# Weighted sums of rows moved from VectorE to TensorE, with the rows loaded back from DRAM

## The chip, the cores and the metric

The kernel runs on one core of one Trainium2 chip. The metric is the device time of one execution in microseconds (us). The engines are called by the profile's letters: PE is TensorE (matrix products and transpositions), DVE is VectorE, ACT is ScalarE, POOL is GpSimd, SP is SyncE, which issues most of the transfers (DMA).

## The reference, cut to what matters

Two transformer layers work on 4 sequences of 512 tokens with 512 features, in float32. The first layer normalizes each row (a row is a token) and gives the result, `xn`, to an attention and to a mixture of experts. This attention has a local window and a compressed memory. The change lies in the making of the compressed memory:

```
w_log   = (xn @ Wcmp + bcmp).reshape(B, C, 4)          # C = 128 groups of 4 tokens
w_cmp   = softmax(w_log, axis=-1)
entries = einsum('bcr,bcrh->bch', w_cmp, xn.reshape(B, C, 4, 512))
ck = apply_rope(rmsnorm(entries @ Wk + bk, kn_w), block_ends)
cv = entries @ Wv + bv
sc = einsum('bhsd,bcd->bhsc', q, ck) * scale            # top 8 of these are attended to
```

Every group of four successive tokens gets four weights that add up to 1, and an entry is the weighted sum of the four rows. From the entries come compressed keys `ck` and values `cv`, 128 for each sequence, which all 16 heads of that sequence use.

## The kernel before

The first layer is a loop of 32 steps (L1020): 8 groups of two heads, and for each group the 4 sequences, here called batches. A step makes the scores and the context of its two heads and at the same time the projections of the next step. `project` (L638) makes these with seven products of half matrices in the place of eight; their sums and differences of blocks are made by DVE and POOL and, for the first four steps, stored to DRAM as `xsd` (L656). Products land in banks of PSUM, which are asked for by tag: three banks are `mm` (projections `p`, outputs `op`), three `sc` (scores, `st`, contexts, the product `wB`), two `tr` (transpositions).

`start_sequence` (L871) normalizes a block of 128 rows: `bn_stats` on DVE, a power on POOL, the scaled rows `xn` on DVE or ACT. It stores `xn` to the DRAM tensor `xnd` (L237; blocks 4 to 7 from ACT's queue, the others from SP's), and turns it by TensorE into `xnT`, which has the features in the partitions (L242, L243). The first batch's four blocks are made ahead of the loop, the second batch's too, the third's in step 0 and the fourth's in step 1. `layernorm` pins the statistics of blocks 0 to 3 to their place in the order (L219).

`compress(b, pool)` (L578) is a generator in four parts, run for batch 0 ahead of the loop (L1007 to L1018) and for batches 1 to 3 in steps 0 to 2 at four places each (L885). Its input `row_w[b]` holds the logits, made by `first_logits` in four column blocks of 32 (L252) and copied to `lr` by ACT (L254).

- Part 1 turns the logits (`wt`), makes the softmax of four (`w1`), and spreads it: `wd[:, :, r]` is the identity times the weight of token r of the group (four DVE instructions, L596).
- Part 2 multiplies `wd` by a matrix of ones (L599), so that bank `wB` holds all 512 weights in every partition. Then for each of the 4 blocks of features DVE multiplies `xnT` by `wB` (L603) and adds up each four neighbours (L604) into `entT`, features in the partitions.
- Part 3 makes keys and values from `entT` in eight products (`kv`, L609), normalizes and rotates the keys.
- Part 4 turns the keys (`trck`, L619) into `ckT` (L620), which the scores `sp` of the step need (L744).

The order of each engine's instructions is made when the kernel is built, from the order of the program and from the build's own estimate of when each instruction can start; what stands in `keep_in_program_order` keeps its place. At run time every engine and every queue works strictly in its order: an instruction that waits holds up all behind it. That the build changes the order can be seen in the trace: the stores of row blocks 8 and 9, written in step 0 behind the four stores of that step's sums, stand ahead of them on SP's queue.

The setup tiles (pool `sp0`, compression's tiles among them) are released after the last compression, at the end of step 2 (L891); the routing of the experts takes their place and starts in step 3.

Of the kernel before, what the change touches and what calls it, by code (L numbers as in the profile page):

```python
# [12 lines left out]
F32 = mybir.dt.float32  # L13
I32 = mybir.dt.int32
AF = mybir.ActivationFunctionType
ALU = mybir.AluOpType
AX = mybir.AxisListType
# [3 lines left out]
P = 128  # L21
B, S, HID = 4, 512, 512
T = B * S
NT = T // P
TC = S // P
KC = HID // P
NH, D = 16, 128
RATIO = 4
C = S // RATIO
# [20 lines left out]
def two_layers(ctx: ExitStack, tc: tile.TileContext, a: dict, out: bass.AP, large: bass.AP):  # L50


    FEW = 32
    nc = tc.nc
    V, G, A, PE = nc.vector, nc.gpsimd, nc.scalar, nc.tensor
# [14 lines left out]
    sp0 = setup.enter_context(tc.tile_pool(name="setup", bufs=2, side="right"))  # L70


    def psum(tag, name):
        return ps.tile([P, 512], F32, tag=tag, name=name, bufs={"mm": 3, "sc": 3, "tr": 2}[tag])
# [53 lines left out]
    xnT = keep.tile([P, KC, T], F32, tag="xnT", name="xnT")  # L128
    x_v = a["x"].rearrange("(n p) h -> p n h", p=P)

    xnd = dram.tile([T, HID], F32, tag="xnd", name="xnd")
# [43 lines left out]

    ident = const.tile([P, P], F32, tag="ident", name="ident")
    make_identity(nc, ident)
    nhalf = const.tile([P, 8], F32, tag="nhalf", name="nhalf")
    G.memset(nhalf, -0.5)
    A.activation(small.tile([P, 8], F32, tag="warm", name="warm", bufs=1), nhalf, AF.Exp)  # L180
    ones_sq = const.tile([P, P], F32, tag="ones_sq", name="ones_sq")
    G.memset(ones_sq, 1.0)
# [376 lines left out]
    def squares(x, n, pool, name, extra=1.0):  # L559

        sq = pool.tile([P, D], F32, tag="sq", name=f"sq_{name}", bufs=1)
        ss = small.tile([P, n], F32, tag=f"ss{n}", name=f"ss_{name}", bufs=4)
        for h in range(n):
            A.activation(sq, x[:, h, :], AF.Square, accum_out=ss[:, h : h + 1])  # L564
        G.tensor_scalar(ss, ss, D * 1e-6, extra, ALU.add, ALU.mult)
        G.tensor_tensor(ss, ss, nhalf[:, 0:n], ALU.pow)  # L566
        return ss

    def rotate(x, tt1, tt2, n, pool, name):

        r1 = pool.tile([P, n, R], F32, tag="r1", name=f"r1_{name}", padded_shape=[P, 6, R] if n > 1 else None, bufs=1)
        r2 = pool.tile([P, n, R], F32, tag="r2", name=f"r2_{name}", padded_shape=[P, 6, R] if n > 1 else None, bufs=1)
        V.tensor_tensor(r1, x[:, :, 0:R], tt1, ALU.mult)
        V.tensor_tensor(r2[:, :, 0:32], x[:, :, 32:R], tt2[:, :, 0:32], ALU.mult)
        V.tensor_tensor(r2[:, :, 32:R], x[:, :, 0:32], tt2[:, :, 32:R], ALU.mult)
        V.tensor_tensor(x[:, :, 0:R], r1, r2, ALU.add)

    def compress(b, pool):  # L578

        w_row = row_w[b]  # L580

        wt = psum("tr", f"wt_{b}")
        for r in range(RATIO):
            PE.transpose(wt[:, ts(r, P)], w_row.rearrange("p (c r) -> p r c", r=RATIO)[:, r, :], ident)
        w1 = pool.tile([P, RATIO], F32, tag="w1", name=f"w1_{b}", bufs=1)
        V.tensor_reduce(w1, wt.rearrange("p (r k m) -> p r k m", k=KC, m=FEW)[:, :, :, 0], AX.X, ALU.add)
        V.tensor_scalar(w1, w1, bcmp[:, 0:1], None, ALU.add)
        mx = pool.tile([P, 1], F32, tag="wmx", name=f"wmx_{b}", bufs=1)
        V.tensor_reduce(mx, w1, AX.X, ALU.max, negate=True)
        sm = pool.tile([P, 1], F32, tag="wsm", name=f"wsm_{b}", bufs=1)  # L590
        A.activation(w1, w1, AF.Exp, bias=mx, accum_out=sm)
        V.reciprocal(sm, sm)
        V.tensor_scalar(w1, w1, sm, None, ALU.mult)
        wd = pool.tile([P, C, RATIO], F32, tag="prod", name=f"wd_{b}", bufs=1)
        for r in range(RATIO):
            V.tensor_scalar(wd[:, :, r], ident, w1[:, r : r + 1], None, ALU.mult)  # L596
        yield
        wB = psum("sc", f"wB_{b}")
        PE.matmul(wB, lhsT=ones_sq, rhs=wd.rearrange("p c r -> p (c r)"), start=True, stop=True)  # L599
        entT = pool.tile([P, KC, C], F32, tag="entT", name=f"entT_{b}", bufs=1)  # L600
        for k in range(KC):
            prod = pool.tile([P, C, RATIO], F32, tag="prod", name=f"prod_{b}_{k}", bufs=1)
            V.tensor_tensor(prod.rearrange("p c r -> p (c r)"), xnT[:, k, ts(b, S)], wB, ALU.mult)  # L603
            V.tensor_reduce(entT[:, k, :], prod, AX.X, ALU.add)  # L604
        yield
        kv = psum("sc", f"kv_{b}")
        for i, w in enumerate((wk, wv)):
            for k in range(KC):
                PE.matmul(kv[:, ts(i, D)], lhsT=entT[:, k, :], rhs=w[:, k, :],  # L609
                          start=(k == 0), stop=(k == KC - 1))  # L610
        V.tensor_tensor(cv[:, b, 0:D], kv[:, ts(1, D)], bkv[:, 1, :], ALU.add)
        ck = pool.tile([P, 1, D], F32, tag="ck", name=f"ck_{b}", bufs=1)
        V.tensor_tensor(ck[:, 0, :], kv[:, ts(0, D)], bkv[:, 0, :], ALU.add)
        ss = squares(ck, 1, pool, f"ck_{b}")
        rotate(ck, t1c, t2c, 1, pool, f"ck_{b}")
        A.activation(ck[:, 0, :], ck[:, 0, :], AF.Copy, scale=ss[:, 0:1])
        yield
        tr = psum("tr", f"trck_{b}")
        PE.transpose(tr[:, 0:C], ck[:, 0, :], ident)  # L619
        A.activation(ckT[:, b, :], tr[:, 0:C], AF.Copy, scale=turned[:, 0:1])  # L620
        yield
# [231 lines left out]
    lg0 = lg1 = const.tile(full, F32, tag="lg", name="lg")  # L853
    row_w = {}
    comp = [compress(b, sp0) for b in range(B)]

    def first_logits(b):
# [581 lines left out]
    for g in range(NG):  # L1439
        b, j = groups1[g]  # L1440
# [743 lines left out]
```

## Time and profile before

| what | value |
| --- | --- |
| median of 3 runs (lowest to highest) | 2073.92 us (2073.34 to 2074.24) |
| the profiled execution | 2074.66 us |
| its span in the profile | 2072.6 us |
| mean granted clock of TensorE | 0.995 |
| DMA | 267.23 MB, 129 GB/s in the mean |
| first and last `wt` (the first instruction of compression) | 27.5 and 158.0 us |
| first and last `kv` | 49.3 and 185.6 us |
| `xnd<-xn` from SP and from ACT, to landing | 2.0 and 2.2 us (median) |

The profile shows one execution by the hardware's own records. The page gives each engine's busy time, the span in 40 slices and the costliest groups of instructions. Queries of the trace give windows (busy time of every engine, granted clock of TensorE and share of the DMA engines in a stretch of time), timelines (start, length, instruction and, in brackets, the idle time before it with what ended it), tiles (every instruction that reads or writes a tile) and the chain of waits (followed back from the last instruction). A float32 product is two passes on TensorE, a transposition is one; pipelined instructions overlap in the lists, so the cost of one is better read from the start of the next.

### The profile page before, as it was taken

How to read it: one execution, taken by the hardware profiler on the slowest of the kernel's cores; microseconds unless marked ns; L12 is line 12 of the kernel's file. 1: busy time of each engine (PE TensorE's matmuls, PEld its weight loads, DVE VectorE, ACT ScalarE, POOL GpSimd, SP SyncE). 2: the span in 40 equal slices, each digit the busy share in tenths (PEclk: the TensorE clock that was granted, in tenths of full speed). 3: DMA queues.
4: the chain of work that ended last, by engine and by line, in shares of the span. 5: the costliest groups of instructions: out<-in, count | busy, mean ns of one | idle time of the engine just before them, and what ended most of it. 6: DMA issues, size and time to landing. Idle time of an engine off the chain costs nothing.

```text
span 2072.6 us, 27984 instructions
## 1 busy us (share of the span) xinstructions
PE 2017.7 (97%) x9130; PEld 1205.3 (58%) x9130; DVE 1452.0 (70%) x3543; ACT 867.9 (42%) x2600; POOL 754.3 (36%) x761
## 2 busy tenths in 40 slices
PE   6999999999999999999999999999999999999997
PEld 4666666666666666666666666666334445445442
DVE  7888967666766666676667778787596555557775
ACT  4554444444444443444444455454243432333332
POOL 4422244443423333344333444353114332332550
PEclk9999999999999999999999999999999999999999
DMA  7102133333333343234443222121317765773551
GB/s 250 68 31 62 42 118 120 143 108 103 130 130 104 109 155 103 92 135 166 183 170 116 70 76 85 42 72 62 119 51 244 263 243 196 257 243 123 158 163 52
DMA packets 98906, 267.23 MB, mean 129 GB/s; under 512 B 14400, under 2 KB 27840, under 8 KB 87488
## 3 DMA queue, kind: packets, MB, share of 16 engines
q0 software_dynamic: 27072, 148.91, 21.4%
q1 hardware_dynamic: 70528, 114.34, 16.4%
q10 hardware_dynamic: 1152, 2.10, 0.3%
q8 instruction: 75, 1.23, 0.2%
q14 instruction: 79, 0.65, 0.1%
HBM read 222.05 MB, written 42.73 MB: 128 GB/s over the span
## 4 chain that ended last, share of the span: by engine, by line
PE 81%; DVE 8%; ACT 3%; POOL 2%; DMA 2%; issue 1%; SPq 0%; ACTq 0%; POOLq 0%; DVEq 0%
PE p L661 23%; PE hp_r L518 12%; PE op L828 10%; PE st L753 4%; PE st L1224 3%; PE qp L1200 3%; PE sp L744 3%; PE cx L1238 2%; PE ca L797 2%; PE o L1307 2%; PE trm_r L506 2%; PE vp L1160 1%; PE trq L681 1%; PE trk L687 1%; PE cc L800 1%
## 5 line engine op out<-in xcount | busy, mean ns | idle before, releaser
L828 PE MATMUL op<-Wo,cT 128*128 128x512 f32 x512 | 230.6, 598 | 5.3 <-DVE lv L725 2.9
L518 PE MATMUL hp_r<-we_r,xT_r 128*128 128x512 f32 (+1 forms) x592 | 224.8, 596 | 0.0
L470 POOL DMA_INDIRECT xr_r<-xnd,rows_r x72 | 89.4, 1242 | 331.6 <-PE trm_r L506 298.2
L761 POOL TENSOR_TENSOR lT<-lT,lmask 128x512 f32<-128x512 f32 (+1 forms) x128 | 157.6, 1244 | 140.8 <-ACT lT L757 140.6
L661 PE MATMUL p<-wT,x 128*128 128x384 f32 x512 | 179.6, 493 | 0.5 <-DVE wT L119 0.5
L661 PE MATMUL p<-wB,x 128*128 128x384 f32 x512 | 175.9, 488 | 4.0 <-DVE u L717 4.0
L661 PE MATMUL p<-wA,xnT 128*128 128x384 f32 x512 | 174.0, 492 | 0.2 <-DVE u L696 0.2
L828 PEld LDWEIGHTS op<-Wo,cT 128*128 128x128 f32 x512 | 92.0, 190 | 115.0 <-issue 77.2
L564 ACT ACTIVATE sq<-qb 128x128 f32<-128x128 f32 x384 | 118.9, 310 | 93.0 <-DVE qb L710 44.9
L1226 ACT ACTIVATE pT<-st 128x1024 f32<-128x1024 f32 x128 | 123.7, 1014 | 62.7 <-PE st L1224 57.0
L518 PEld LDWEIGHTS hp_r<-we_r,xT_r 128*128 128x128 f32 (+1 forms) x592 | 83.8, 170 | 97.3 <-issue 91.8
L831 DVE TENSOR_TENSOR acc<-acc,op 128x512 f32<-128x512 f32 x128 | 87.4, 685 | 69.4 <-PE op L828 69.0
L661 PEld LDWEIGHTS p<-wB,x 128*128 128x128 f32 x512 | 93.9, 190 | 68.5 <-issue 10.2
L661 PEld LDWEIGHTS p<-wT,x 128*128 128x128 f32 x512 | 94.5, 193 | 63.5 <-issue 6.7
L661 PEld LDWEIGHTS p<-wA,xnT 128*128 128x128 f32 x512 | 95.6, 193 | 61.0 <-issue 2.9
L675 ACT ACTIVATE qb<-qb,ss 128x128 f32<-128x128 f32 x256 | 81.9, 390 | 110.7 <-POOL ss L566 108.6
L508 ACT COPY xT_r<-trm_r 128x512 f32<-128x512 f32 x72 | 41.8, 581 | 198.0 <-PE hp_r L518 188.3
L757 ACT ACTIVATE lT<-st,ss 128x256 f32<-128x256 f32 (+1 forms) x128 | 47.2, 449 | 175.4 <-PE st L753 175.3
L753 PE MATMUL st<-qkT 128*128 128x256 f32 (+1 forms) x512 | 110.4, 357 | 0.0
L534 POOL DMA_INDIRECT row_r<-yd,slot_r x64 | 74.2, 1160 | 94.0 <-DVE row_r L1341 35.8
L753 PEld LDWEIGHTS st<-qkT 128*128 128x128 f32 x512 | 93.1, 193 | 11.4 <-issue 1.4
L566 POOL TENSOR_TENSOR ss<-ss,nhalf 128x6 f32<-128x6 f32 x64 | 95.7, 1496 | 5.3
(360 smaller groups left out, 4334.2 us busy)
## 6 DMA issues: line engine op xcount, KB each, us to landing
x<-xsd SPq DMA_DIRECT2D x112, 256.0 KB, 3.1
yd<-yr_r SPq DMA_DIRECT2D x72, 256.0 KB, 3.4
wA<-in_wA SPq DMA_DIRECT2D x16, 384.0 KB, 3.6
wB<-in_wB SPq DMA_DIRECT2D x16, 384.0 KB, 7.6
xnd<-xn SPq DMA_DIRECT2D x24, 256.0 KB, 2.0
accd<-acc SPq DMA_DIRECT2D x18, 256.0 KB, 2.0
acc<-in_x SPq DMA_DIRECT2D x16, 256.0 KB, 4.9
Wo<-in_Wo SPq DMA_DIRECT2D x8, 512.0 KB, 3.6
```

The source lines that it names most:

```text
L470: G.indirect_dma_start(out=out, out_offset=None, in_=src, in_offset=at_rows(idx))
L518: PE.matmul(hp[ts(h, m), :], lhsT=xT[:, k, ts(h, m)], rhs=w[:, ts(k, HID)], start=(k == 0), stop=(k == KC - 1))
L534: G.indirect_dma_start(out=x, out_offset=None, in_=self.yd, in_offset=at_rows(self.r.slot[:, k, n : n + 1]))
L564: A.activation(sq, x[:, h, :], AF.Square, accum_out=ss[:, h : h + 1])
L566: G.tensor_tensor(ss, ss, nhalf[:, 0:n], ALU.pow)
L661: PE.matmul(p, lhsT=x[:, k, ts(c, P)], rhs=w[:, k, :], start=(k == 0), stop=(k == 1))
L675: A.activation(x[:, j, :], x[:, j, :], AF.Copy, scale=sq[t][:, j : j + 1])
L753: PE.matmul(st[:, ds((t % 2) * 256, n)], lhsT=qkT[:, HG + h, ts(t, P)], rhs=qkT[:, h, ds(t * P, n)], start=True, stop=True)
L761: G.tensor_tensor(dst, dst, lmask.rearrange("p a w j -> p (a w j)")[:, 0:n], ALU.mult)
L828: PE.matmul(op, lhsT=cT[:, h, ts(t, P)], rhs=wo[:, h, :], start=(h == 0), stop=(h == HG - 1))
L831: V.tensor_tensor(acc[:, n, :], acc[:, n, :], op, ALU.add)
L1226: A.activation(pt[:, ts(pair, 2), :], st, AF.Exp, scale=SCALE1)
```

## The change

Part 2 of `compress` is made in another way. The rows of the batch are loaded back from `xnd` with the tokens in the partitions, as `rows4` (4 blocks of 128 tokens, 1 MB, on SP's queue). A constant `fold` is the sum of the four 32-column blocks of the identity, so `fold[p, c]` is 1 where p and c agree modulo 32. The weights are spread over `fold` instead of the identity: `wd` has 32 x 4 columns in the place of 128 x 4. Turned by TensorE and copied by ACT it becomes `wsel`: its column block n picks, for the 32 groups of token block n, each group's four tokens with their weights. Four products with 32 columns each, one for each block of tokens, give the entries in one bank, groups in the partitions. ACT copies them (`ent`, in the buffer of `lr`), TensorE turns them in four blocks, and ACT copies the result to `entT`. The remaining parts are as before. The layer's statistics keep the pins they had: the diff does not touch them.

```diff
+    fold = sp0.tile([P, FEW], F32, tag="fold", name="fold", bufs=1)
     nhalf = const.tile([P, 8], F32, tag="nhalf", name="nhalf")
     G.memset(nhalf, -0.5)
+    G.tensor_tensor(fold, ident[:, ts(0, FEW)], ident[:, ts(1, FEW)], ALU.add)
+    for n in (2, 3):
+        G.tensor_tensor(fold, fold, ident[:, ts(n, FEW)], ALU.add)
...
         w_row = row_w[b]
+        rows_ = pool.tile([P, TC, HID], F32, tag="rows4", name=f"rows4_{b}", bufs=1)
+        nc.sync.dma_start(out=rows_, in_=xnd[ts(b, S), :].rearrange("(n p) h -> p n h", p=P))
...
-        wd = pool.tile([P, C, RATIO], F32, tag="prod", name=f"wd_{b}", bufs=1)
+
+        wd = pool.tile([P, FEW, RATIO], F32, tag="wd", name=f"wd_{b}", bufs=1)
         for r in range(RATIO):
-            V.tensor_scalar(wd[:, :, r], ident, w1[:, r : r + 1], None, ALU.mult)
+            V.tensor_scalar(wd[:, :, r], fold, w1[:, r : r + 1], None, ALU.mult)
         yield
-        wB = psum("sc", f"wB_{b}")
-        PE.matmul(wB, lhsT=ones_sq, rhs=wd.rearrange("p c r -> p (c r)"), start=True, stop=True)
+        tr = psum("tr", f"trw_{b}")
+        PE.transpose(tr[:, 0:P], wd.rearrange("p c r -> p (c r)"), ident)
+        wsel = pool.tile([P, P], F32, tag="wd", name=f"wsel_{b}", bufs=1)
+        A.copy(wsel, tr[:, 0:P])
+
+        ep = psum("sc", f"ent_{b}")
+        for n in range(TC):
+            PE.matmul(ep[ts(n, FEW), :], lhsT=wsel[:, ts(n, FEW)], rhs=rows_[:, n, :], start=True, stop=True)
+        ent = pool.tile([P, HID], F32, tag="lr", name=f"ent_{b}", bufs=1)
+        A.copy(ent, ep)
+        tr = psum("tr", f"tre_{b}")
+        for k in range(KC):
+            PE.transpose(tr[:, ts(k, C)], ent[:, ts(k, P)], ident)
         entT = pool.tile([P, KC, C], F32, tag="entT", name=f"entT_{b}", bufs=1)
-        for k in range(KC):
-            prod = pool.tile([P, C, RATIO], F32, tag="prod", name=f"prod_{b}_{k}", bufs=1)
-            V.tensor_tensor(prod.rearrange("p c r -> p (c r)"), xnT[:, k, ts(b, S)], wB, ALU.mult)
-            V.tensor_reduce(entT[:, k, :], prod, AX.X, ALU.add)
+        A.copy(entT, tr.rearrange("p (k c) -> p k c", k=KC))
         yield
```

## The prediction

> **What bounds the kernel now.** I read the page first, for the shares of the engines and the forty slices, then the busy time in short windows over the first 280 us, because the trace shows all four compressions there (the tile view of `prod`: 46.6 to 174 us).
>
> ```profile
> PE 2017.7 (97%) x9130; PEld 1205.3 (58%) x9130; DVE 1452.0 (70%) x3543; ACT 867.9 (42%) x2600; POOL 754.3 (36%) x761
> ...
> PE   6999999999999999999999999999999999999997
> ```
>
> TensorE is busy 97% of the span. So time taken from VectorE counts only where TensorE stands idle for it. In the windows TensorE idles 15.2 us in 0:40 (loads, the first normalization, tables), which this change does not touch; 1.2 us in 40:60; 3.1 us in 60:200; 4.5 us in 200:280, where VectorE works on the routing. Next, the work that goes, from the view of one tile:
>
> ```profile
> L603 DVE TENSOR_TENSOR prod<-xnT,wB x16: 670/680/689, 46.6 to 172.4; 128x512 f32<-128x512 f32 x16
> L604 DVE TENSOR_REDUCE entT<-prod x16: 653/678/689, 47.7 to 173.5; 128x128 f32<-128x512 f32 x16
> ```
>
> Sixteen pairs at 0.68 us each. Then the timeline of TensorE and the windows of 2 us around its gaps (columns: length, busy and count of PE, PEld, DVE, ACT, POOL; granted clock; DMA share; GB/s):
>
> ```profile
> 43.62 1.02 PE L599 MATMUL wB<-wd,ones_sq 128*128 128x512 f32 x2
> 44.48 1.45 PE L661 MATMUL p<-wB,x 128*128 128x384 f32 x4
> ...
> 60.65 0.33 PE L619 MATMUL trck<-ident,ck 128*128 128x128 f32 x1 [1.48 <-ACT ck L616]
> ...
> 117.99 1.10 PE L599 MATMUL wB<-wd,ones_sq 128*128 128x512 f32 x2 [1.01 <-DVE wd L596]
> ...
> 166.60 1.10 PE L599 MATMUL wB<-wd,ones_sq 128*128 128x512 f32 x2 [1.25 <-DVE wd L596]
> ```
>
> ```profile
> 58.00:60.00 2.00, 1.18 (x4) 0.38 (x2) 2.00 (x9) 0.50 (x3) 0.81 (x2) 1.00 0.39 139
> 60.00:62.00 2.00, 1.32 (x10) 1.09 (x11) 2.00 (x6) 1.55 (x8) 0.24 (x1) 1.00 0.34 131
> 62.00:64.00 2.00, 2.00 (x9) 1.73 (x9) 1.54 (x11) 0.21 (x1) 1.92 (x3) 0.59 0.35 131
> 64.00:66.00 2.00, 2.00 (x9) 1.73 (x9) 2.00 (x10) 1.56 (x5) 1.63 (x2) 0.55 0.08 32
> ```
>
> The reader is to see one place where compression holds up TensorE: at 59.2 it has nothing left to do until batch 0's compressed keys are turned (`trck`), while VectorE is full. After that gap the granted clock falls to 0.59 and 0.55. The chain of waits prices it: the same eight passes of `st` take
>
> ```profile
> 62.69 2.99 PE st L753 x8
> ...
> 68.69 1.52 PE st L753 x8
> ```
>
> so 1.47 us are lost in `st`, 0.36 in `sp` before it (1.25 against 0.89) and 0.11 in `trk` after it: 1.9 us.
>
> **The change, part by part.**
>
> *VectorE, removed.* Per batch 4 x (0.68 + 0.68) = 5.4 us. The four `wd` (0.33 us each at 128x128) become 128x32; nearest row of that size, the turn of `ck` (128x32), 0.18: another 0.6. Together 6.0 per batch, 24 us in all. For batches 1 to 3 the `kv` products stand at 92.2, 138.6 and 183.4 us, while the last `entT` is ready at 80.7, 126.3 and 174.2; nothing on TensorE waits for `entT` there. So most of the 24 us buy nothing by themselves.
>
> *TensorE, added.* The `wB` product goes: its successor starts 0.85 us later. In comes a product of four 32-column blocks with 512 columns streamed, the shape of the logits (`lg_r`, eight passes, successor 0.99 us later): +0.14. One transposition of `wd` and four of `ent`: four transpositions in a row take 0.44 (`trx` in the chain of waits), so 5 x 0.11 = 0.55. Per batch +0.69, in all **+2.8 us**, and on the path, since TensorE is the bound and nothing hides it.
>
> *The gap at 59 us, removed.* Batch 0's `kv` waited for VectorE's products, done at 54.7. In the new chain, with the rows there at 46.8 (below): product 1.0, copy 0.59 (row of `lr_r`), four transpositions 0.6, copy 0.58 (row of `xnT`), that is 49.6 plus hand-overs, about 50.5; then sixteen `kv` passes of 0.11, 52.3 instead of 57.9. The keys then take 3.5 us (57.9 to 61.4 before), so they are ready near 56, before the products of step 1 run out at 59.2. Gap 1.5 us, its clock 1.9, and the 0.4 us of small waits in 44:48: **-3.8 us**. What is late next is TensorE itself, with the evictions of `p` behind it. If the gap stays, this term is 0.
>
> *The waits for `wd` at 118 and 166 us.* 2.3 us in all; the four smaller `wd` end about 0.5 earlier each time: **-1.1** (0 if the build moves the transposition forward by as much; -2.3 if they go).
>
> *The bank of `wB`.* It is held through all eight VectorE instructions, and `cc` of the context waits for it ("PEld cc" 1.1 us in two places). TensorE works on during most of it: I take 0, at best -1.1. Against that stand two more users of the two `tr` banks, about 1 us each.
>
> *ScalarE, added.* Three copies: 128x128, nearest row 0.37 (`ckT`), and twice 0.58: 1.5 per batch. ScalarE is busy 9 to 13 of 20 us from 40 to 240, which hides them, but TensorE waits for two of them in its fixed order. The logits have the same hop (product, copy of 0.59, transpositions) and lost 0.7 us once and nothing in the next three batches. In 40:44 ScalarE is busy 3.8 of 4 us, so batch 0's first copy may come late. Bounds 0 and, with one queued normalization (0.81) and a pair of squares (0.5) ahead of each of eight hops, 10 us; nearest is the logits row: inside the 1.0 taken below. No gain is possible, for nothing is taken off.
>
> *SyncE, added: the rows.* Four loads of 1 MB, 0.4 us of issue each. Each waits until its batch's rows have landed in DRAM, batches 1 to 3 also until the product before has released the tile.
>
> ```profile
> 36.51 4.49 SPq L656 DMA_DIRECT2D xsd<-x  x4
> 41.05 0.98 SPq L93 DMA_DIRECT2D wB<-in_wB  x2
> ```
>
> In the program batch 0's load is written after these sums and before that load of weights, and the queue kept this order here, so it is issued at 41.0 to 41.4. Loads of 1 MB landed 5.4 (`pw`) to 10.1 us (`woT`) after issue: 46.8 with the nearest in load, 51.5 at the worst. TensorE comes to the product at 45.8 (the slot of `wB`, then four passes of `p`); behind it in TensorE's queue stand `trq`, `trk` and the `p` of this step, and VectorE's evictions wait for these. I take a wait of **+1.0 us**, between 0 (the build issues the load before the sums) and 5.7. Behind the load on the queue stand `wB` and both biases of the next group, 3 us later; GpSimd waits for one of these at 48.4 and would start its next key scaling (52.3 before) at about the old time. For the others: batch 1's load can go at about 48 and is needed at 72, batch 2's at 92 to 97 and needed at 118, batch 3's at 122 and needed at 167. Their cover is 20 us or more. Stores queued behind them wait some 2 us, and nothing reads those soon.
>
> [...]
>
> *GpSimd, added.* Three additions of 128x32; nearest row `t2c`, 0.46: 1.4 us, in its idle 2.57 us before 4.69. At the worst they delay the first rows by 1.4.
>
> [...]
>
> **Sum:** +2.8 - 3.8 - 1.1 + 1.0 = -1.1 us. The profiled execution took 2074.66 us (span 2072.6 and 2.1 around it), so 2073.5; it lies 0.7 above the median of the runs, 2073.92. On that scale the forecast is **2072.8 us**: a change within 0.2% (4.1 us), which is about what a measurement of this kernel can tell from none. Its own range, 2069.9 to 2077.
>
> **Rivals.**
>
> *The rows come late (slower).* TensorE stands at batch 0's product until the load lands. If the load goes behind `wB` and the biases (1.15 MB, issued until 43.1), it lands near 52: a wait of 6.2, then a spell of low clock, 1.9. 2.8 + 6.2 + 1.9 - 3.8 = +7.1: **2081**. It decides from a landing at about 48 on, where the sum passes +4 if the clock falls too. For it: DMA is full from 42 to 48 us (shares 0.9 to 1.0). Against: the order of the queue above.
>
> *The order opens up (faster).* TensorE's idle time in 40:200, 4.4 us, and the 1.9 of clock all go, and with VectorE ahead and the `sc` bank free, half of the 4.5 us in 200:280 too: -8.6 + 2.8 = -5.8: **2068**. For it: VectorE is at 17.8 to 19.1 of 20 us in 40:80. Against: routing can begin only when the setup tiles are released, at 193 us.
>
> *It does nothing for the gap.* VectorE's freed time is filled with later work, and the keys come as late. 2.8 + 1.0 - 1.1 = +2.7: **2076.6**, again within 0.2%.
>
> **How the numbers follow.** Forecast 0.45, rows late 0.24, order opens 0.20, nothing for the gap 0.11. Faster by over 0.2%: the third and a little of the first, 0.23; slower: the second and a sixth of the last and some tail of the first, 0.29; within: 0.48. The range reaches from the faster case with 2 us more (2066) to the late rows with 2 us more (2083); that takes in the upper bound of the copies (10 in place of the 1.0: +7.9, 2082).
>
> **What would show it.** Right: no gap near 59 us and clock 1.00 from 40 on; `ep` (in the place of `wB`) released by a DMA with a wait near 1 us; about 2.8 us more TensorE work; VectorE 24 us less busy with the time hardly moved. Wrong: a wait over 3 us for `rows4` or for a copy; a new spell of low clock; routing earlier than its steps; or a difference that arises after 280 us, from an order that the build has changed elsewhere.

## The result, and the profile after

The changed kernel takes **2079.11 us** (median of 14 runs, 2077.92 to 2081.20); the kernel before, run beside it on the same chip, took 2074.07. The ratio is 1.0022, with a 95% interval of 1.0015 to 1.0029: slower by some 5 us. The forecast was 2072.8. The time lies inside the range given, but it moved the other way, and by a little more than the 0.2% that the prediction called no change. The profiled execution took 2079.24 us (span 2077.4, clock 0.997).

First the page of the changed kernel:

```profile
PE 2016.3 (97%) x9174; PEld 1202.6 (58%) x9174; DVE 1433.6 (69%) x3511; ACT 873.0 (42%) x2612; POOL 754.4 (36%) x764
...
PE   6899999999999999999999999999999999999987
```

VectorE is 18.4 us less busy than before (1452.0 then; 24 were forecast), and TensorE is at 97% as it was. Next, the windows over the old gap and the stretch behind it (columns as in the prediction):

```profile
58.00:60.00 2.00, 1.39 (x9) 0.29 (x9) 2.00 (x8) 2.00 (x6) 0.67 (x2) 1.00 0.04 9
60.00:62.00 2.00, 1.89 (x15) 1.84 (x16) 2.00 (x5) 1.88 (x11) 0.09 (x1) 1.00 0.74 278
62.00:64.00 2.00, 2.00 (x17) 1.90 (x15) 1.85 (x8) 1.83 (x7) 1.83 (x3) 1.00 0.66 247
64.00:66.00 2.00, 2.00 (x17) 1.92 (x17) 2.00 (x12) 1.49 (x5) 2.00 (x2) 1.00 0.39 143
```

The spell of clock 0.59 and 0.55 at 62 to 66 us (from here on: the spell) does not occur here. The timeline of TensorE in the changed kernel shows what happened to the gap, and what came after it (the entry in brackets is the idle time before the instruction and what ended it):

```profile
47.93 2.20 PE L677 MATMUL p<-wA,xnT 128*128 128x384 f32 x6 [0.72 <-DVE lv L741]
50.07 1.07 PE L613 MATMUL ent<-rows,wsel 128*32 128x512 f32 x8
...
58.34 1.06 PE L257 MATMUL lg_r<-xnT,wr 128*32 128x512 f32 x8 [1.10 <-ACT xnT L248]
59.64 0.33 PE L635 MATMUL trck<-ident,ck 128*128 128x128 f32 x1 [0.23 <-ACT ck L632]
...
68.50 0.55 PE L795 MATMUL trs<-ident,s 128*128 128x128 f32 x3 [0.91 <-ACT s L786]
...
72.71 0.30 PE L607 MATMUL trw<-ident,wd 128*128 128x128 f32 x1 [1.72 <-DVE wd L604]
...
92.58 1.56 PE L677 MATMUL p<-wB,x 128*128 128x384 f32 x4 [1.11 <-DVE u L733]
```

The wait of `trck` shrank from 1.48 to 0.23 us, and the product of the entries did not wait for its rows. But five waits stand here that the kernel before does not have at these places: for `lv`, `xnT`, `s`, `wd` and `u`, 5.6 us together. Summed over the whole stretch in which compression runs, the windows give this (kernel before first, then the changed one):

```profile
40.00:200.00 160.00, 155.66 (x764) 105.42 (x761) 137.09 (x396) 84.69 (x283) 52.41 (x67) 0.99 0.20 68
```

```profile
40.00:200.00 160.00, 152.71 (x795) 103.11 (x794) 114.89 (x355) 89.01 (x291) 49.55 (x65) 1.00 0.28 94
```

TensorE idles 4.3 us of the 160 before and 7.3 after: 3.0 us more, with VectorE 22 us less busy. To see where the difference arises I compare the start of one and the same TensorE instruction, a turn of queries late in layer 0 (before, changed, and one of the experiments below, later2):

```profile
1093.96 0.60 PE L681 MATMUL trq<-ident,qb 128*128 128x128 f32 x4
```

```profile
1097.47 0.60 PE L697 MATMUL trq<-ident,qb 128*128 128x128 f32 x4
```

```profile
1094.27 0.60 PE L697 MATMUL trq<-ident,qb 128*128 128x128 f32 x4
```

I call this start **the mark**. It is 3.5 us later after the change. The same shift stands from about 200 us to 1400 us; it arises in the first four steps and nowhere else in this layer. The rest of the 4.8 us of span appears behind 1400 us, in code that the change does not touch. The traces of this case, one execution of each kernel, differ there by up to 3 us where the code is the same, so the mark is the finer measure of what an edit does, and the ratio of the timed runs the surer one. The mark has chance in it too: at part 2's first product near 43 us, ahead of most of the edits, the traces already stand between 1.4 us ahead of the kernel before (loads) and 1.9 us behind it (passes20).

### The profile page after: what moved, and what is told of

Same layout as the page of the kernel before. It is cut to its first block, busy times and chain, and to the rows that moved or that the text cites. A ratio compares the mean times of both kernels' runs of the same rounds, so it can differ in the third digit from the quotient of the medians.

```text
span 2077.4 us, 28060 instructions
## 1 busy us (share of the span) xinstructions
PE 2016.3 (97%) x9174; PEld 1202.6 (58%) x9174; DVE 1433.6 (69%) x3511; ACT 873.0 (42%) x2612; POOL 754.4 (36%) x764
## 4 chain that ended last, share of the span: by engine, by line
PE 76%; DVE 8%; ACT 3%; POOL 3%; issue 2%; DMA 1%; ACTq 0%; POOLq 0%; DVEq 0%
PE p L677 22%; PE hp_r L523 12%; PE op L844 10%; PE st L769 4%; PE qp L1216 3%; PE st L1240 3%; PE sp L760 2%; PE cx L1254 2%; PE ca L813 2%; PE trm_r L511 2%; PE o L1323 1%; DVE pS L1260 1%; PE vp L1176 1%; PE trq L697 1%; PE cb L816 1%
```

## The experiments

The theories by the letters that the expectations use. **A**: VectorE's queue, in which row statistics moved into the freed time wait for their buffer. **A'**, after A's first form fell: the queue is refilled with later work, so that step 0's results come late. **B**: TensorE's added passes. **C**: the loads from DRAM. **H**: the chain of hops (copies by ScalarE). **P**: the weights' VectorE instructions standing still beside GpSimd's masks. **Q**: VectorE's queue is full whatever is in it. **R**: idle time of TensorE is conserved. **O**: the place at which the new part 2 stands in the queues. Each ratio is to the kernel before, run on the same chip, with its 95% interval; the marks are relative to 1093.96.

### The halves of the change, the loads, and the statistics' buffers

loads: the kernel before, with the load of `rows4` added at the head of `compress`.

> The kernel before, with the four loads of rows added and not used. Theories A and B: within 1 us of the kernel before. Theory C: +2 us or more.

Ratio 1.0006 (0.9997 to 1.0015), mark -1.55. C falls. The negative mark is not shown to be a gain from loads: at `trck` (59.70 against 60.65) this execution is 1.0 us ahead already, and the spell does not occur in it (last section). At batch 1's `wt` it is 2.6 us ahead (63.43 against 66.07), at batch 1's first `kv` only 1.6 (90.54 against 92.16); in between TensorE waits 0.56 us for `wd` at 69.65, where the kernel before does not wait.

b0: `if b == 0:` around the new way, the old one otherwise. b123: the reverse.

> The new way for batch 0 alone, batches 1 to 3 as before. Theory A: the aggregation's wait for ScalarE at 46 to 56 us stays (over 3 us), and with it most of the loss: +2 to +4 us on the kernel before. Theory B: a quarter of the passes, +0.7, less what the gap at 59 us gives: -1 to +0.7. Theory C: +1.2.

> The new way for batches 1 to 3, batch 0 as before. Theory A: no aggregation waits in 40:60; what is left is three times the added passes less the smaller waits for wd, 0 to +2 us on the kernel before. Theory B: +2 to +4. Theory C: +3.7.

b0 1.0017 (1.0008 to 1.0026), mark +1.37; b123 1.0024 (1.0012 to 1.0035), mark +2.24. Both halves lose. That the marks add up nearly to the whole change's 3.51 says little: the times do not add up (0.17% and 0.24% against 0.22%), and neither half has the spell, which the kernel before has. In b0, where only the gap was attacked, the gap's wait went as in the full change and TensorE's idle time in 40:200 rose from 4.3 to 7.7 us. The largest new wait stands at batch 1's part 2, which b0 makes as before (timeline of b0):

```profile
73.35 1.12 PE L630 MATMUL wB<-wd,ones_sq 128*128 128x512 f32 x2 [2.08 <-DVE wd L627]
```

mv12: the changed kernel, with twelve buffers for the statistics of the blocks that ScalarE scales. VectorE's aggregates had waited for a buffer 5.1 us in 36:110.

```diff
-        mv = small.tile([P, 2], F32, tag="mv", name=f"mv_{n}")
+        mv = pool.tile([P, 2], F32, tag="mv0", name=f"mv_{n}", bufs=12) if scaled else small.tile(...)
```

> The changed kernel, but blocks 4 to 15 have 12 buffers for their row statistics (mv) instead of sharing 3. Theory A (VectorE's queue: the build moves the statistics' aggregation into the freed time, where it stands and waits for a buffer that ScalarE's normalization frees, 5.1 us in 36:110, and everything behind it comes late): the wait of L228 for ScalarE goes to 0, TensorE's waits for wd and s in step 0 (1.7 and 0.9) shrink, and the time falls by 2 to 5 us, to within 1.5 us of the kernel before (2072 to 2075.5). Theory B (TensorE's added passes, 4 x 0.69 = 2.8 us, are the loss): the time stays 2.5 to 5 us above the kernel before. Theory C (the loads from DRAM): stays 5 above.

Ratio 1.0039 (1.0025 to 1.0053), mark +5.62. The wait for buffers was gone and the kernel slower still. TensorE now ran into this (timeline of mv12, then its windows):

```profile
72.34 0.30 PE L607 MATMUL trw<-ident,wd 128*128 128x128 f32 x1 [3.46 <-DVE wd L604]
```

```profile
70.00:72.00 2.00, 0.00 (x0) 0.00 (x0) 2.00 (x3) 0.72 (x4) 1.99 (x2) 1.00 0.19 69
72.00:74.00 2.00, 1.66 (x7) 0.56 (x11) 1.53 (x5) 1.14 (x3) 0.00 (x0) 0.81 0.04 8
74.00:76.00 2.00, 2.00 (x10) 0.62 (x3) 0.00 (x0) 0.89 (x2) 0.00 (x0) 0.50 0.34 131
```

VectorE is full (2.00 of 2.00) while TensorE stands at the first instruction of batch 1's part 2, and the clock falls behind it. A as first posed falls. before_mv12, the control:

> The kernel before with twelve buffers for the row statistics of the blocks scaled by ScalarE, the control of the same edit in the changed kernel, which had cost 1.9 us there. Theory A': no row statistic waited for a buffer in the kernel before, so within 1 us of it. Theory B and H: as A'. If it costs 2 us here too, more buffers let the build move the statistics forward in both kernels.

Ratio 0.9998 (0.9989 to 1.0007), but mark +2.21: there TensorE waited 2.7 us for `wd` at 72 us. So the times show no cost in the old kernel, and the one trace shows the same spot giving way.

### Passes alone, relief alone

passes and passes20: the kernel before, with 5 or 20 unread transpositions per batch ahead of `entT`.

```diff
+        tr = psum("tr", f"tre_{b}")
+        for k in range(5):
+            PE.transpose(tr[:, ts(k % KC, C)], xnT[:, k % KC, ds(b * S, P)], ident)
```

> The kernel before, and in each batch five transpositions more, of a block of xnT into a bank of the turns, whose result nobody reads. Theory B: 4 x 0.55 = 2.2 us more in layer 0, a ratio of 1.0011. Theory A': TensorE idles 4.4 us in 40:200, so some of the passes fall into its gaps, and 0 to 2.2 us are lost; what is above comes from the bank that they take. Theory H: as A'.

> The kernel before with twenty unread transpositions in each batch in the place of the five of the earlier run, which had cost 1.2 us at the end of layer 0 in the trace and 4.0 (1.7 to 5.4) in the times. Theory B: 80 x 0.11 = 8.8 us, less at most 2 for gaps that they fill, so 2081 to 2083. If the passes were hidden by idle time of TensorE: under 5.

passes 1.0017 (1.0008 to 1.0026), that is 3.5 us (1.7 to 5.4), mark +1.07; passes20 1.0053 (1.0039 to 1.0067), 11.0 us (8.1 to 13.9), mark +12.3. The marks need the start taken off them: the first `wB` product, ahead of which no pass is added, starts at 43.62 us before, at 42.79 in passes and at 45.49 in passes20. From there to the mark passes loses 1.9 us for 2.2 us of added passes (0.11 each), passes20 10.4 us for 8.8. Added passes are paid at about their length or more; idle time hides little or nothing of them.

nosums: the kernel before, with the sixteen pairs on VectorE replaced by one ScalarE copy for each batch (the weighted sums are left out).

```diff
-            V.tensor_tensor(prod.rearrange("p c r -> p (c r)"), xnT[:, k, ts(b, S)], wB, ALU.mult)
-            V.tensor_reduce(entT[:, k, :], prod, AX.X, ALU.add)
...
+        A.copy(entT, xnT[:, :, ts(b, S)].rearrange("p k (c r) -> p k c r", r=RATIO)[:, :, :, 0])
```

> The kernel before without the multiplications and sums of the weighted rows on VectorE (left out: the weighted sums; ScalarE copies every fourth column of xnT instead). It frees 21.7 us of VectorE and adds no TensorE pass and three hops fewer. Theory A': the freed time is refilled and TensorE idles at other places; layer 0 gains under 1.5 us. Theory B: the relief works and only the passes took it back: layer 0 gains 3 to 5 us, 2069 to 2071. Theory H: as B, for the three hops are missing.

Ratio 1.0004 (0.9995 to 1.0013), mark -0.40. VectorE is relieved of all sums, no pass is added, and no time is won. Its TensorE idles 6.7 us in 40:200 where the kernel before idles 4.3 (loads, which has no spell either, 5.4). B's sum for this run (3 to 5 us gained) is wrong, that of A' (under 1.5) right. Relief for nothing and passes paid give 2.8 us and more of the change's 5; that they are not the whole account is shown by later2 below, which has both.

pin: the changed kernel, with all blocks' statistics held in program order.

```diff
-        pin(V.bn_stats(st, acc[:, n, :]))
+        (tc.keep_in_program_order if scaled else pin)(V.bn_stats(st, acc[:, n, :]))
```

> The changed kernel with the row statistics of all sixteen blocks held in program order. Theory A' (after the change VectorE's queue is refilled from later work, row statistics first, so that in step 0 the weights wd, the scores' s and the turned rows come late and TensorE idles at 58 to 73 us): the waits of TensorE for wd, s and xnT in 36:100, 4 us together in the changed kernel, fall below 2 and the time is 2075 to 2077. Theory B (the added TensorE passes, 2.8 us, are the loss, and the gap at 59 us was worth little): within 0.5 us of the changed kernel's 2079. Theory H (the chain of copies on ScalarE is the loss): the waits stay, 2079.

Ratio 1.0103 (1.0088 to 1.0119), mark +19.2; the waits of TensorE in pin begin with

```profile
PE trx L247 <- ACT xn L239: 12.7, 7, 4.9
```

Every theory missed it by far. Held in place, the row blocks come late for their turns, which costs far more than the statistics' waits did. It says nothing for or against A', since it makes a new wait of its own.

### The weights' chain, and the product's shape

In the changed kernel three of the weights' VectorE instructions in step 0 are far longer than in other steps, beside GpSimd's masks (last section). wact and before_wact move them to ScalarE, in the changed kernel and in the one before.

```diff
-        V.tensor_scalar(w1, w1, bcmp[:, 0:1], None, ALU.add)
...
-        V.tensor_scalar(w1, w1, sm, None, ALU.mult)
+        A.activation(w1, w1, AF.Copy, scale=sm)
...
-            V.tensor_scalar(wd[:, :, r], fold, w1[:, r : r + 1], None, ALU.mult)
+            A.activation(wd[:, :, r], fold, AF.Copy, scale=w1[:, r : r + 1])
```

> The changed kernel with the weights' last steps on ScalarE: the product with the reciprocal and the four products with fold are activations with a scale, and the addition of bcmp, which the softmax cancels, is left out. Theory P (in step 0 three VectorE instructions of the weights stand still while GpSimd multiplies a mask: 0.96, 0.81 and 0.98 us for usual 0.22, 0.22 and 0.24, 2.1 us in all, and TensorE waits for wd for that reason): TensorE's waits for wd, 2.5 us in the changed kernel, fall below 0.8, layer 0 is 1 to 2 us shorter, 2077 to 2078. Theory Q (VectorE's queue is full from 56 to 73 us whatever is in it, and the weights are late because of what stands ahead of them): the five instructions less bring under 0.7 us, and the wait stays above 1.5. Theory B (only the passes count): 2079, the idle time moves to another place.

> The same edit in the kernel before, where wd has 512 columns and ScalarE needs some 0.37 us for each quarter. There TensorE waits for wd 2.3 us at 118 and 167 us. Theory P: these waits fall by the longest of the sixteen products, 1.45 us for usual 0.33, layer 0 gains 1 to 2 us, 2072 to 2073. Theory Q: under 0.7 us gained. Theory B: within 0.5 us of before, since idle time taken from one place comes back at the next.

wact 1.0030 (1.0018 to 1.0042), mark +5.1; before_wact 1.0006 (0.9997 to 1.0015), mark +1.1. P falls as the cause of the loss: the waits for `wd` did fall, from 2.5 to 1.0 us, but the wait moved one hop on, and nothing was won (timeline of wact):

```profile
73.65 1.07 PE L612 MATMUL ent<-rows,wsel 128*32 128x512 f32 x8 [1.29 <-ACT wsel L608]
```

direct: the product with the features in the partitions at once, which saves a copy and four transpositions.

```diff
+        for k in range(KC):
+            for n in range(TC):
+                PE.matmul(ep[:, ds(k * C + n * FEW, FEW)], lhsT=rows_[:, n, ts(k, P)], rhs=wsel[:, ts(n, FEW)], start=True, stop=True)
```

> The changed kernel with the entries made straight with the features in the partitions: sixteen products of 128 x 128 with 32 columns take the place of the four products, ScalarE's copy of ent and the four transpositions. Theory B: the time follows TensorE's passes. If a pass of 32 columns costs as little as a quarter of one with 128 (0.03), layer 0 gains 0.4 per batch; at 0.11 as for kv, it loses 32 x 0.11 - 1.4 = 2.1 per batch, 2087. Theory H (the hops cost): one hop less gains up to 1 us for each batch at the same passes.

Ratio 1.0094 (1.0079 to 1.0109), mark +17.8, where B's dear end gave 2087. The 32 passes of batch 1 take 3.76 us in the timeline, 0.12 each, where a pass of `kv` with 128 columns takes 0.11 to 0.12: here a pass of 32 columns was as dear as one of 128. The time is some 6 us above B's dear end, and B had no term for what else the trace shows: the clock falls during these passes or right behind them in three of the four batches, to 0.50 at the first (last section). H is not tested cleanly by this run. One point speaks for a share of it: in the changed kernel ScalarE, in its order, stood 1.49 us for `ent` and 1.31 us for `tre` at 50 to 53 us, and VectorE then waited 3.44 us for ScalarE's next `xn`. later2 has the same 3.44, and not the loss.

### The place of part 2

The new part 2 of batch 1 begins at 71 us in TensorE's queue, and its `entT` is needed by `kv` at 94.8 us. The old part stood there too; its `entT` was ready 11.5 us ahead of `kv` (80.7 and 92.2). The new one needs about 5 us with its hops. later2 and later3 put the part of batches 1 to 3 one or two places later; b123_later2 does the first with batch 0 as before the change.

```diff
-        for t in (0, 1, 3.5, 4):
+        for t in (0, 2, 3.5, 4):
             jobs0.append(((b - 1, t), lambda b=b: next(comp[b])))
```

> The changed kernel with the new part 2 of batches 1 to 3 one place later in its step (behind the second head's turn of s), still some 15 us ahead of kv. Theory O (the lost time is in the order of the queues: the part stands where the kernel before needed it for 5.4 us of VectorE, and TensorE comes to it before wd is there): the waits for wd, 2.5 us, go and layer 0 ends 1.5 to 2.5 us earlier than in the changed kernel, 2076.5 to 2077.5. Theory R (idle time of TensorE is conserved at the start of layer 0: what one wait gives up, a chain on VectorE and ScalarE takes back at the next): TensorE's named waits in 36:300 stay at 7 to 8 us and the time at 2079.

> As the run before it, two places later (behind the turn of the first head's context). Theory O: as there, unless entT now comes late for kv, which stands about 8 us behind. Theory R: 2079.

> The new part 2 for batches 1 to 3 alone, one place later, batch 0 as before the change. At the old place it cost 2.2 us at the end of layer 0, of which 3 x 0.69 = 2.1 are passes. Theory O: the waits for wd (1.6 us) go, so 0.3 to 0.9 remain, 2075 to 2075.5. Theory R: 2.2 us as before, 2077.

later2 1.0005 (0.9996 to 1.0014), mark +0.31; later3 1.0021 (1.0012 to 1.0031), mark +3.56; b123_later2 1.0003 (0.9994 to 1.0012), mark -0.61. With one number changed, 3.2 of the 3.5 us come back at the mark, more than O's 1.5 to 2.5, and 3.5 us in the times (0.22% against 0.05%, each against the kernel before, run beside it). R's 2079 falls, though a part of the waiting did come back elsewhere: TensorE's idle time in 40:200 went from 7.3 only to 5.0 us, with new waits for `entT` (0.9) and `sT` (0.65). In the timeline of later2 the turn of `wd` stands at 79.43 and waits for nothing (no bracket):

```profile
76.84 2.75 PE L677 MATMUL p<-wT,xnT 128*128 128x384 f32 x8
79.43 0.27 PE L607 MATMUL trw<-ident,wd 128*128 128x128 f32 x1
79.53 0.81 PE L677 MATMUL p<-wB,x 128*128 128x384 f32 x2
80.40 1.06 PE L613 MATMUL ent<-rows,wsel 128*32 128x512 f32 x8
```

`wd` is ready at about 72.4 in later2, as it was in the changed kernel; TensorE now does its projections and contexts first: the first `ca` of the context starts at 71.48, where in the changed kernel it stands behind the turn and starts at 74.65. The `u` of step 0, for which TensorE waited 1.1 us at 92, has no wait here either. In later3 the turn and the product fall so close together that TensorE waits for ScalarE's copy between them, 3.0 us in two places: O's own warning (too late) came from another link of the chain than `kv`.

later2_mv12 and b123_later2_mv12 add the twelve buffers:

> The changed kernel with both edits: part 2 of batches 1 to 3 one place later, and twelve buffers for the row statistics. Alone, the first took layer 0 from 3.5 to 0.4 us behind the kernel before, the second made it 5.7. Theory O (the place of the part was the loss; the buffers brought TensorE to it still earlier, where it stood 3.5 us and the clock fell): with the part moved the buffers now help: the wait of VectorE's row statistics goes, and of TensorE's waits those for xnT, s and lv (2.7 us) shrink by 1 to 2.5; layer 0 ends 0.5 to 2 us ahead of the kernel before, 2072.5 to 2075. Theory R: as much new waiting elsewhere, 2075 to 2077; if the buffers cost by themselves: 2077.5.

> The same two edits with batch 0 made as before the change. Twelve buffers in the kernel before left a wait of 2.7 us for wd at 72 us; here the part stands later. Theory O: layer 0 within 1 us of the run without the buffers (0.5 us ahead of the kernel before), 2074 to 2076, since the gap at 59 us stays. Theory R: as there. If it is well below the other run, the new way is worth nothing for batch 0 even with the place mended.

later2_mv12 1.0002 (0.9993 to 1.0011), mark +0.60; b123_later2_mv12 0.9998 (0.9989 to 1.0007), mark +2.5. The buffers no longer cost (with the old place they had cost 2.1 at the mark), and TensorE's idle time in 40:200 falls from 5.0 to 3.1 us, as O said. The mark did not follow: against later2, 1.5 us are already lost at the first `trw` (44.40 against 42.86); the other 0.7 I can't place. None of the four kernels with the part one place later can be told from the kernel before; none beats it.

One control is missing: the kernel before with its own part 2 one place later. It had room for that, as said, and its waits for `wd` at 118 and 166 us (2.3 us) might have gone as well. So the runs show that the changed kernel loses its time at this place; they do not show that the old part stood at the best place.

## Why the prediction was wrong

**VectorE's relief buys nothing by itself**: right; nosums wins nothing. Its size was 18.4 us instead of 24. **TensorE's passes, +2.8**: right in size. In the trace the entries' eight passes run 50.07 to 51.06 and the four transpositions take 0.43; passes and passes20 confirm that such work is paid. **The rows, +1.0**: the wait was 0, but by luck. The load was issued at 41.36 us, as forecast, and landed 7.3 us later, at 48.6 (the other three landed after 5.5 to 5.7); that is past the 48 from which the prediction saw the rows come late. The build had put the product behind ten more passes of `p`, at 50.07 instead of 45.8. **GpSimd and SyncE**: hidden, as forecast. **ScalarE's copies**: no product of TensorE waits for one of the three in 36:200. A new spell of low clock did not come: the clock is 1.00 in every window of 2 us from 36 to 240.

**The step that failed is "The gap at 59 us, removed", at its last sentence: "What is late next is TensorE itself, with the evictions of `p` behind it."** Of the gap's wait 1.25 of 1.48 us went. I took the -3.8 us as a gain to the end, without following TensorE to the next instruction in its fixed order that needs something of a chain which had not become shorter. How the gain was lost can be seen at two instructions of batch 1, the turn of the logits (`wt`) and the first `kv`, in the kernel before, the changed one and later2; ahead of each stands the same work of TensorE, but for the change's own passes:

```profile
66.07 0.64 PE L584 MATMUL wt<-ident,lr_r 128*128 128x128 f32 x4
92.16 0.39 PE L609 MATMUL kv<-wk,entT 128*128 128x128 f32 x2
```

```profile
63.45 0.65 PE L591 MATMUL wt<-ident,lr_r 128*128 128x128 f32 x4
94.84 0.39 PE L625 MATMUL kv<-wk,entT 128*128 128x128 f32 x2
```

```profile
63.24 0.64 PE L591 MATMUL wt<-ident,lr_r 128*128 128x128 f32 x4
91.82 0.39 PE L625 MATMUL kv<-wk,entT 128*128 128x128 f32 x2
```

The changed kernel is 2.6 us ahead at the first and 2.7 behind at the second. Between them TensorE waits for `s` (0.91), for `wd` of batch 1 at the old place of part 2 (1.72) and for `u` (1.11), and makes 0.7 us of added passes; some 0.9 us I can't place. later2, with the part one place later, waits there for `s` alone of the three and loses half as much: with the waits for `wd` and `u`, 3.2 us of the loss at the mark are gone. That the loss arises at this place is shown, not argued. b0 shows that it takes no new part 2: with only batch 0 changed, TensorE waits 2.08 us for the old `wd` of batch 1.

The wait for `wd` has two parts. In the kernel before (VectorE, then TensorE):

```profile
70.29 0.92 DVE L596 TENSOR_SCALAR wd<-ident,w 128x128 f32<-128x128 f32 x4
71.46 1.02 PE L599 MATMUL wB<-wd,ones_sq 128*128 128x512 f32 x2
```

There `wd` was done at 71.2 and TensorE came at 71.46. In the changed kernel TensorE comes at 70.99, 0.5 earlier, and `wd` is done at 72.6, 1.4 later. `wd` hangs on the logits, the softmax and VectorE's sorting of the scores. The softmax's reciprocal starts at 69.63 us in both kernels, so that chain had not become shorter. Behind it the weights' instructions took 1.1 us longer, beside GpSimd (last section), and one instruction of the sorting stands ahead of `wd`.

Three of the five new waits are not of the old place: those for `lv`, `xnT` and `s`, 2.7 us, stand in later2 and b0 as they do here, and not in b123. They come with batch 0's new way and eat up the 1.25 us won at the gap. With twelve buffers (mv12) only 0.46 of them is left.

**The waits for `wd`, -1.1**, failed with it: 2.3 us before, 2.5 after. The wait at 118 went and that at 167 fell from 1.25 to 0.80, but a new one of 1.72 came at 72.7, where the prediction had no term: there the four smaller `wd` ended 1.4 us later, not 0.5 earlier. The aside's bound of 0 came nearest by its number, not by its reason.

**The clock's 1.9 us** were mis-sized as a sure gain. Six of the nine kernels that keep the gap's wait have no spell behind it (last section), so its absence here can't be put down to the gap's removal. And it does not reach the end whole: loads, with the gap and without the spell, is as far ahead at `wt` as the changed kernel (2.6 us) and has lost 1.0 of it again at `kv`. Against loads the change costs 3.51 + 1.55 = 5.1 us at the mark, and passes and idle time in 40:200 (7.3 against 5.4) give 2.8 + 1.9 = 4.7. These are sums over single executions; the timed runs say 5.0 (3.1 to 6.0).

Of the rivals none took place. "It does nothing for the gap" had the right sign, and its reason, freed VectorE time filled with later work, fits nosums, but here the gap did go. The rows landed later than forecast (48.6 instead of 46.8), but ahead of the place at which the build had put their product. What stays open: why `u` is no longer late in later2, why the mark of later2_mv12 does not follow its idle time, and the differences of up to 3 us behind 1400 us.

## What to carry to other kernels

When a gap of the bounding engine closes, follow that engine to the next instruction of its fixed order that needs another engine, and ask whether that chain has become shorter too; if it has not, the gain ends there. When a part gets cheaper on one engine, try a new place for it in the order: here a single place later gave back 3.5 of the 5 us, which left no difference from the kernel before that could be told. And an engine that is not the bound can be relieved of some 20 us for nothing (nosums), while passes added to the bound are paid (passes, passes20: 10.4 us for 8.8 in the larger).

## What the runs showed of the hardware

**The same gap does not always cost clock.** Nine kernels have TensorE's wait of 1.48 to 1.57 us for `ck` near 60 us (in one, nosums, at 56). In three of them (before, passes, b123_later2_mv12) the clock then falls to 0.50 to 0.68 for some 4 us; in the other six it stays at 1.00 behind this wait. The windows behind the gap in loads:

```profile
60.00:62.00 2.00, 1.98 (x16) 1.69 (x15) 1.63 (x4) 0.66 (x3) 1.11 (x2) 1.00 0.28 105
62.00:64.00 2.00, 2.00 (x17) 1.90 (x15) 2.00 (x18) 1.17 (x4) 2.00 (x2) 1.00 0.07 26
```

The wait of loads ended at 59.70, and the clock is 1.00 behind it; the kernel before shows 0.59 and 0.55 at 62 to 66, behind the same wait. Why the clock fell behind three of these nine waits and stayed at 1.00 behind the other six, no run shows.

**In direct the clock also falls with no gap.** There TensorE makes 32 passes with 32 columns streamed from 50.07 us on, and no idle time shows from 46 to 60 us (two of the windows):

```profile
52.00:54.00 2.00, 2.00 (x17) 1.97 (x17) 0.72 (x2) 0.24 (x1) 2.00 (x2) 0.91 0.76 289
54.00:56.00 2.00, 2.00 (x4) 1.01 (x3) 0.00 (x0) 1.05 (x2) 1.20 (x2) 0.50 0.69 194
```

The clock is lower again around the passes of the third and the fourth batch (in the mean 0.91 in 120:140 and 0.83 in 180:200; there waits of 0.6 and 0.8 us stand ahead of the passes), and not at the second (1.00 in 60:80 and in 80:100). The third batch's 32 passes take 4.15 us, where the second's took 3.76.

**Three of the weights' small VectorE instructions took some four times as long beside GpSimd.** Timelines of the changed kernel, VectorE and then GpSimd:

```profile
66.59 0.96 DVE L594 TENSOR_SCALAR w<-w,bcmp 128x4 f32<-128x4 f32 x1
...
70.02 0.81 DVE L600 TENSOR_SCALAR w<-w,wsm 128x4 f32<-128x4 f32 x1
...
71.14 1.42 DVE L604 TENSOR_SCALAR wd<-fold,w 128x32 f32<-128x32 f32 x4
```

```profile
65.04 2.48 POOL L777 TENSOR_TENSOR lT<-lT,lmask 128x512 f32<-128x512 f32 x2
...
69.53 2.54 POOL L777 TENSOR_TENSOR lT<-lT,lmask 128x512 f32<-128x512 f32 x2 [0.82 <-ACT lT L773]
```

The addition for four columns takes 0.96 us for usually 0.22, and it ends (67.55) as the mask does (67.52). The product with the reciprocal takes 0.81 for 0.22, and the longest of the four `wd` 0.98 for 0.24; GpSimd's second pair of masks runs beside both (69.53 to 72.07). The traces show them side by side; no run shows why. That it makes `wd` late is not excluded; but in wact, with these instructions on ScalarE, no time was won (mark +5.1, where the changed kernel has +3.5).
